# Turning a group's result tile by tile in four column groups of TensorE (graph layers, 4096 nodes)

## The chip, the cores and the metric

One Trainium2 chip; the program runs on one of its cores. The time is the device time of one execution in microseconds, and the median of the runs is quoted. Engines are named as in the profile: PE is TensorE (PEld its weight loads), DVE is VectorE, ACT is ScalarE, POOL is GpSimd, SP is SyncE, which here only issues DMA transfers.

## The reference

Two graph layers on 4096 nodes with 512 features, each on the layer norm of its input and added to it. The change lies in the second layer (layer 1), attention with 8 heads of 64 (argument names as in the call):

```python
# layer 0
h = jnp.maximum(_layernorm(x, axis=-1), 0.0)
node_att = jax.nn.softmax(h @ node_w, axis=0)
he = h @ edge_w
edge_att = jax.nn.softmax(jnp.where(adj > 0, he @ he.T, NEG_BIG), axis=1)
x = x + adj * (node_att * edge_att) @ (h @ weight) + bias
# layer 1
h = jnp.maximum(_layernorm(x, axis=-1), 0.0)
data1 = (h @ W.T + b).reshape(N, H, D)
src = jnp.einsum('nhd,xhd->nh', data1, src_proj)
trg = jnp.einsum('nhd,xhd->nh', data1, trg_proj)
e = src.T[:, :, None] + trg.T[:, None, :]
e = jnp.where(e >= 0, e, 0.01 * e)
e = e + adj[None, :, :]
scores = jax.nn.softmax(e, axis=-1)
out = jnp.einsum('hnm,hmd->hnd', scores, data1.transpose(1, 0, 2))
x = x + out.transpose(1, 0, 2).reshape(N, H * D)
```

So for each head and each of 4096 rows there is a weighted sum over 4096 neighbours and a denominator, and the result is their quotient plus the layer's input.

## The kernel before

Layer 0 takes the first 1580 us or so and isn't touched. Layer 1 works in eight **groups**: four blocks of 1024 rows (`WL`) times two halves of the heads (`HG` = 4 heads). A group has 32 **steps**, one for each tile of 128 neighbours (`m`, 0 to 31). The neighbours lie on the partitions and the rows along the free dimension, so the products come out turned: 128 partitions (head and feature) by rows.

The order is written out by hand (`manual_schedule`): line 1400 lists the stages of a step with how many steps ahead each works, and each engine and DMA queue runs its own instructions in the order in which they are issued. In step `s`:

- `load` (4 ahead): SP fetches a 128x1024 tile `e` of the adjacency.
- `exps` (1 ahead): ACT writes `ex`, the exponential of `e`, to PSUM. There is one buffer of `ex`, so ACT writes it only when DVE has read the one before.
- `rest`: at the first step of a group ACT copies what is left of the last group's sums out of PSUM (`copy_rest`, lines 1252 to 1258), after `os[0][0]` was copied at the end of `gather`.
- `weigh` (1 ahead): DVE forms the four heads' weights `pr` (lines 1171, 1174), in the order 3, 0, 1, 2 (`ORDER`). Head 3 uses `e3`, a second exponential; the others use `ex`. `pr` has two buffers for heads 1 to 3 and three for head 0. In one step of four (`BY_LOG`: m = 3, 7, ...) head 0's weights come from ACT and POOL (`lg`), and DVE has three products instead of four.
- `factors` (2 ahead): ACT writes `e3` (line 1114) and, for head 0, `rl` (line 1140), or `pr` from `lg` (line 1137) for a step in `BY_LOG`. `logs` (4 ahead) writes `lg` (line 1120).
- `scale`: in the first two groups, ACT (before, POOL) also multiplies two heads of the values by `d_m` (line 1100).
- `gather`: PE adds the step's products to the sums. Every product has a stationary operand at most 32 columns wide, so four products, one in each **column group** of 32 columns, go into the four quarters of PSUM's partitions: 16 products of values (line 1208, `pv`) and four of denominators (line 1213, `dn`). In the seven steps of `BY_HALF` one more product goes into a single column group; the order `cols` of the column groups is shifted by one after each, so that they go round. The last step adds nine products of sums that POOL and DMA have gathered (`acc`).

The **end of a group** is worked off during the next group by the generator `finish` (lines 1290 to 1318). `denominators` turns the 512 denominators' copy `od` and picks what is needed by four products with the matrix `pick` (line 1265); DVE takes the reciprocals `rd`. `turn` (lines 1278 to 1282) turns a row tile: two transposes of 128x128, with the whole width of PE. Two row tiles share one PSUM tile `pt` (one buffer). Then ACT scales each head's 64 columns with its share of `rd` into a tile `o` (line 1310, four instructions a row tile), POOL adds the layer's input by DMA (`due`, issued in `weigh` where m mod 4 is 1, from line 1154), and SP stores the two row tiles. `o` has two buffers, of which `od` takes one once a group.

`finish` is advanced by one `yield` in the steps of `PARTS` (lines 1013, 1415), counted in the next group: reciprocal products at 1, reciprocals and the first turn at 2, then, for each pair of row tiles, turns at 2, 6, 10 and 14, the scalings of one tile at 4, 8, 12, 16 and of the other at 5, 9, 13, 17, and the stores at 10, 14, 18 and 22. The last group ends in `finish_last` (lines 1321 to 1360), when nothing else runs: PE turns four tiles, forms the reciprocal products and turns the other four, and DVE and ACT share the scalings.

Of the kernel before, what the change touches and what calls it, by code (L numbers as in the profile page):

```python
# [8 lines left out]
FP = mybir.dt.float32  # L9
AF = mybir.ActivationFunctionType  # L10
ALU = mybir.AluOpType
# [4 lines left out]
P = 128  # L16
# [12 lines left out]
def kernel(  # L29
# [15 lines left out]
    nc = tc.nc  # L45
    N, F = x.shape
    H, D = 8, 64
    HG, WL = 4, 1024
    WT = WL // P
    NT = N // P  # L50
# [7 lines left out]
    ident = const.tile([P, P], FP, name="ident")  # L58
# [4 lines left out]
    x1 = dram.tile([N, F], FP, name="x1")  # L63
# [39 lines left out]
    with tc.tile_pool(name="w0", bufs=1) as wp, tc.tile_pool(name="a0", bufs=2) as ap_, tc.tile_pool(  # L103
        name="a0s", bufs=8
# [75 lines left out]
        def turn(t):  # L180
            b, j = divmod(t, TB)
            if j == 0:
                hts[b] = ap_.tile([P, KC, BL], FP, name="h_t")
            if t >= T0:
                nc.vector.transpose(
                    hts[b][:, :, j * P:(j + 1) * P].rearrange("p k (a q) -> p k a q", q=S),
                    hqs.pop(t).rearrange("p (a k q) -> p k a q", k=KC, q=S))
                return
            h = hs.pop(t)
            pt = pp.tile([P, KC, P], FP, name="bank")  # L190
            for k in range(KC):
                nc.tensor.transpose(pt[:, k, :], h[:, k * P:(k + 1) * P], ident)
            nc.vector.tensor_copy(hts[b][:, :, j * P:(j + 1) * P], pt)
            logit(t, h)
# [291 lines left out]
    with tc.tile_pool(name="mx0", bufs=1) as mx0, tc.tile_pool(name="b_b", bufs=3) as adj0, tc.tile_pool(  # L486
        name="mx1", bufs=1
    ) as mx1, tc.tile_pool(name="b_a", bufs=3) as adj1, tc.tile_pool(name="b_m", bufs=4) as mkp, tc.tile_pool(name="b_s", bufs=2) as sp, tc.tile_pool(
        name="b_p", bufs=6, space=PSUM
# [94 lines left out]
        for n in range(-5, len(items)):  # L584
# [3 lines left out]
            if n >= 0:  # L588
                i, j, t = items[n]
# [10 lines left out]
                if n in more:  # L600
                    f, m = more[n]
# [7 lines left out]
    with tc.tile_pool(name="c_x", bufs=1) as ldx, tc.tile_pool(name="c_y", bufs=1) as ldy, tc.tile_pool(  # L609
        name="c_d", bufs=2  # L610
    ) as wkp, tc.tile_pool(name="c_m", bufs=1) as mxp, tc.tile_pool(name="c_o", bufs=4) as iop, tc.tile_pool(
        name="c_s", bufs=2
    ) as sp, tc.tile_pool(name="c_q", bufs=1, space=PSUM) as p_q, tc.tile_pool(
        name="c_p", bufs=1, space=PSUM
# [12 lines left out]
        steps = [(n, q) for n in range(NB) for q in mixed(n)]  # L627
# [121 lines left out]
        left, scale, norms, zs = [], {}, iter(()), {}  # L749
# [25 lines left out]
        def denominators(n):  # L775
            b = ORDER_B[n]
            sc = sp.tile([P, TB], FP, name="sc")
            nc.vector.tensor_tensor(sc, zs.pop(n), dr[:, b * TB:(b + 1) * TB], ALU.add)
            nc.vector.reciprocal(sc, sc)
            nc.vector.tensor_tensor(sc, sc, na[:, b * TB:(b + 1) * TB], ALU.mult)  # L780
            scale[n] = sc
# [3 lines left out]
        def finish(n, j):  # L785

            b = ORDER_B[n]
            oc = iop.tile([P, F], FP, name="xt")
            blk[n][1].append(oc)
            for c, half in enumerate((2, 3) if j < 2 else (4, 5)):  # L790
                nc.scalar.activation(oc[:, c * F2:(c + 1) * F2], cs_[half][:, (j % 2) * F2:(j % 2 + 1) * F2], AF.Copy,
                                     scale=scale[n][:, j:j + 1])
            nc.gpsimd.dma_start(oc, xb_d[rows_of(b * TB + j), :], accum_op=ALU.add)
# [133 lines left out]
        for s in range(-5, end):  # L927
# [5 lines left out]
            n, q = steps[s]  # L933
# [28 lines left out]
        pt = bank(7)  # L962
# [45 lines left out]
    Q = P // 4  # L1008
# [1 line left out]

    PARTS = (0, 1, 2, 4, 5, 6, 8, 9, 10, 12, 13, 14, 16, 17, 18, 22)
    BY_LOG = (3, 7, 11, 15, 19, 23, 27, 31)
    BY_HALF = (4, 8, 12, 16, 20, 24, 28)
    BY_DMA = [m for m in range(NT - 1) if m not in BY_HALF]
# [2 lines left out]
    with tc.tile_pool(name="p", bufs=2) as prp, tc.tile_pool(name="s0", bufs=1) as s0, tc.tile_pool(  # L1019
        name="za", bufs=1  # L1020
    ) as zp0, tc.tile_pool(name="e", bufs=4) as ep, tc.tile_pool(name="p0", bufs=3) as pr0p, tc.tile_pool(name="rl", bufs=2) as rlp, tc.tile_pool(
        name="io1", bufs=2
    ) as iop, tc.tile_pool(name="s1", bufs=1) as sp, tc.tile_pool(name="e3", bufs=2) as e3p, tc.tile_pool(
        name="zb", bufs=1
    ) as zp1, tc.tile_pool(name="ac", bufs=2) as acp, tc.tile_pool(
        name="os", bufs=1
    ) as osp, tc.tile_pool(name="u", bufs=1) as usp, tc.tile_pool(
        name="p_x", bufs=1, space=PSUM
# [111 lines left out]
            nc.scalar.activation(r, zs_[i, 0], AF.Relu, bias=ngd_m[:, h // HG, m:m + 1], scale=d_m[:, h, m:m + 1])  # L1140
            rl[i, m] = r

        due = []

        def sums(i, m):
            if m < 2:
# [113 lines left out]
        def denominators(i):  # L1260
            os_, od = late.pop(i)
            yield os_
            pd = p_t.tile([P, JT, 2, 4], FP, name="pt")
            for j in range(JT):
                nc.tensor.matmul(pd[:, j, :, :].rearrange("p e r -> p (e r)"), od[:, j * P:(j + 1) * P],  # L1265
                                 pick.rearrange("p e r -> p (e r)"), start=True, stop=True)
            yield
            rd = sp.tile([P, JT, 2, 4], FP, name="rd", bufs=2)
            nc.vector.reciprocal(rd, pd)
            yield rd  # L1270

        def share(rd, t, r):
            q, j = divmod(t, JT)
            k = ORDER[r]
            e, r4 = (0, (k - 1) * HV + q) if k in (1, 2) else (1, (HV if k else 0) + q)
            return rd[:, j, e, r4:r4 + 1]

        def turn(os_, t, pt):
            q, j = divmod(t, JT)
            for c in range(2):  # L1280
                nc.tensor.transpose(pt[:, 2 * c:2 * c + 2, :].rearrange("p k d -> p (k d)"),  # L1281
                                    os_[c][q][:, j * P:(j + 1) * P], ident)

        def part(ap, i, t, n):

            b, g = groups[i]
            t += b * WT
            return ap[t * P:(t + n) * P, g * HG * D:(g + 1) * HG * D].rearrange("(j p) (h d) -> p j h d", p=P, h=HG)

        def finish(i):  # L1290


            dens = denominators(i)
            os_ = next(dens)
            yield
            next(dens)
            yield
            rd = next(dens)
            old = []
            for t in range(0, WT, 2):  # L1300
                pt = p_t.tile([P, 2, HG, D], FP, name="pt")
                for j in range(2):
                    turn(os_, t + j, pt[:, j, :, :])
                if t > 2:
                    nc.sync.dma_start(part(out, i, t - 4, 2), old.pop(0))
                yield
                o = iop.tile([P, 2, HG, D], FP, name="o")
                for j in range(2):
                    for r, k in enumerate(ORDER):
                        nc.scalar.activation(o[:, j, k, :], pt[:, j, r, :], AF.Copy, scale=share(rd, t + j, r))  # L1310
                    if j == 0:
                        yield
                old.append(o)
                due.append(lambda o=o, t=t: nc.gpsimd.dma_start(o, part(x1, i, t, 2), accum_op=ALU.add))
                yield
            nc.sync.dma_start(part(out, i, WT - 4, 2), old.pop(0))
            yield
            nc.sync.dma_start(part(out, i, WT - 2, 2), old.pop(0))
            yield

        def finish_last(i):

# [78 lines left out]
        for s in range(len(steps)):  # L1401
            for f, ahead in stages:
                if s + ahead < len(steps):
                    f(*steps[s + ahead])
                if s == 0 and f is exps:
                    early_logs(0, BY_LOG[0])
            if s == 0:
                ending = iter(())
            elif s == 2:
                ending = tables()  # L1410
            elif s % NT == 0:
                ending = finish(s // NT - 1)
            if s == len(steps) - 2:
                ending = finish_last(len(groups) - 1)
            if s < NT or s % NT in PARTS or s > len(steps) - 3:
                next(ending, None)
        for _ in ending:
            pass

# [33 lines left out]
```

## Time and profile before

| | us |
|---|---|
| median of 3 runs | 2805.27 (2805.01 to 2806.02) |
| the profiled execution, time | 2803.11 |
| its span in the profile | 2801.3 |
| layer 1's first product | 1603.0 |
| layer 1's last product of the main loop starts | 2790.2 |
| granted clock of PE over the span | 0.995 |

| group of instructions | count | mean of one, us |
|---|---|---|
| PE products of values, 128x512 (L1208) | 8192 | 0.594 |
| PE products of denominators with `d_m`, 128x512 (L1213) | 1984 | 0.592 |
| PE transposes `pt<-ident,os`, 128x128 (L1281) | 112 | 0.286 |
| PE reciprocal products `pt<-pick,o`, 128x8 (L1265) | 64 | 0.256 (median) |
| weight loads of 128x32 (L1208) | 8192 | 0.110 |
| weight loads of 128x128 (L1281 / L1265, median) | 112 / 64 | 0.140 / 0.192 |
| DVE `pr` from `ex` (L1174) | 512 | 1.271 |
| DVE `pr` from `e` (L1174) | 256 | 1.356 |
| ACT scalings `o<-pt,rd`, 128x64 (L1310) | 224 | 0.304 |

The span is one execution on the core, seen by the profiler; the time of that execution is 1.8 us more. Instructions on PE overlap: a product is listed with the time from its start to its modelled end, so their durations don't add up, and the distance from one start to the next tells the pace. A plain f32 product is listed as two instructions (4096 products of values in L1208). The same holds, less strongly, of DVE and ACT, where one instruction starts a little before the one before it ends. Times in the views are from the span's start. A bracket at a line's end is the engine's idle time just before it, and the instruction whose end ended it.

### The profile page before, as it was taken

The numbers are of one execution on the slowest core, as the hardware profiler recorded it, in microseconds if no ns is written. First come the engines' busy times: TensorE is split into PE (matmuls) and PEld (weight loads), VectorE is DVE, ScalarE is ACT, GpSimd is POOL, SyncE is SP. The second block draws the span as 40 slices with busy tenths as digits, with TensorE's granted clock in tenths as the row PEclk, the third lists the DMA queues.
The fourth block names the chain that finished last, engine by engine and source line by source line (L and its number), as shares of the span: only waits on it lengthen the run. The fifth ranks groups of instructions, "written<-read, shape, count | busy, mean of one in ns | idle before, by whom it ended". The sixth has DMA issues, their size and how long they took to land. (4 is left out here: it accounts for less than half of the span.)

```text
span 2801.3 us, 46750 instructions
## 1 busy us (share of the span) xinstructions
PE 2753.2 (98%) x16747; PEld 1499.1 (54%) x16747; DVE 2506.5 (89%) x3427; ACT 1475.5 (53%) x2218; POOL 1462.9 (52%) x1234
## 2 busy tenths in 40 slices
PE   7999999999999999999999899999999999999998
PEld 4885444444888888888885333323232323232322
DVE  7877799898888888888886799999999999999998
ACT  2212233333123333433332288998888888888786
POOL 5322344444011010111107698888978797979786
PEclk9999999999999999999999899999999999999999
DMA  5536898888889998999867279999999998989897
GB/s 175 176 104 244 285 330 301 303 297 269 202 200 201 214 262 188 232 251 218 230 193 195 84 193 241 239 229 240 220 241 228 241 231 236 225 244 224 218 218 172
DMA packets 535992, 629.85 MB, mean 225 GB/s; under 512 B 292152, under 2 KB 346456, under 8 KB 535760
## 3 DMA queue, kind: packets, MB, share of 16 engines
q1 hardware_dynamic: 461920, 415.87, 49.2%
q0 software_dynamic: 71824, 207.07, 34.1%
q10 hardware_dynamic: 2016, 3.93, 0.4%
q8 instruction: 131, 2.15, 0.3%
q14 instruction: 101, 0.83, 0.1%
HBM read 404.23 MB, written 107.15 MB: 183 GB/s over the span
## 5 line engine op out<-in xcount | busy, mean ns | idle before, releaser
L1208 PE MATMUL pv<-pr,sup 128*32 128x512 f32 x8192 | 1052.4, 594 | 9.7 <-DVE ngd_m L1163 5.5
L1174 DVE SCALAR_TENSOR_TENSOR pr<-z,g_m,ex 128x1024 f32<-128x1024 f32 x512 | 630.5, 1271 | 6.0 <-PE dn L1213 5.6
L1208 PEld LDWEIGHTS pv<-pr,sup 128*32 128x32 f32 x8192 | 306.7, 110 | 605.4 <-issue 564.3
L1185 POOL TENSOR_TENSOR acc<-acc,pr 128x1024 f32<-128x1024 f32 x240 | 576.0, 2400 | 100.4 <-DVE pr L1174 97.3
L531 PE MATMUL pe<-he_t,he_t 128*128 128x512 f32 x896 | 386.5, 592 | 0.0
L1213 PE MATMUL dn<-pr,d_m 128*2 128x512 f32 x1984 | 385.7, 592 | 0.0
L705 ACT ACTIVATE d<-d 128x1024 f32<-128x1024 f32 x126 | 133.1, 1056 | 430.8 <-DVE d L697 226.5
L1174 DVE SCALAR_TENSOR_TENSOR pr<-z,g_m,e 128x1024 f32<-128x1024 f32 x256 | 347.2, 1356 | 0.7 <-ACT e L1114 0.4
L1104 ACT ACTIVATE ex<-e 128x1024 f32<-128x1024 f32 x256 | 263.2, 1028 | 157.2 <-DVE pr L1174 156.1
L1114 ACT ACTIVATE e<-e,ld_m 128x1024 f32<-128x1024 f32 x256 | 291.1, 1137 | 0.0
L531 PEld LDWEIGHTS pe<-he_t,he_t 128*128 128x128 f32 x896 | 169.4, 190 | 208.3 <-issue 193.7
L744 PE MATMUL po<-he_t,at 128*128 128x256 f32 x1024 | 262.9, 379 | 1.0 <-ACT he_t L755 1.0
L744 PE MATMUL po<-sup,u 128*128 128x256 f32 x1024 | 263.3, 380 | 0.0
L1171 DVE SCALAR_TENSOR_TENSOR pr<-rl,ngd_m,ex 128x1024 f32<-128x1024 f32 x191 | 242.7, 1271 | 3.2 <-ACT ex L1104 2.6
L744 PE MATMUL po<-sup,at 128*128 128x256 f32 x1024 | 243.7, 381 | 1.0 <-DVE mc L537 1.0
L1140 ACT ACTIVATE rl<-z,ngd_m,d_m 128x1024 f32<-128x1024 f32 x191 | 234.8, 1229 | 0.0
L831 POOL DMA_DIRECT2D he_t<-he_t x56 | 48.7, 939 | 355.9 <-ACT he_t L747 301.9
L715 DVE TENSOR_TENSOR at<-d,a 128x1024 f32<-128x1024 f32 x126 | 154.1, 1223 | 84.0 <-PE po L744 46.3
L744 PEld LDWEIGHTS po<-sup,at 128*128 128x128 f32 x1024 | 195.7, 191 | 27.9 <-issue 1.2
L744 PEld LDWEIGHTS po<-he_t,at 128*128 128x128 f32 x1024 | 194.6, 190 | 27.6 <-issue 1.4
L744 PEld LDWEIGHTS po<-sup,u 128*128 128x128 f32 x1024 | 194.1, 190 | 25.9
L536 POOL DMA_DIRECT2D er_d<-mk x136 | 74.2, 546 | 234.0 <-DVE rm L533 217.8
(272 smaller groups left out, 3925.9 us busy)
## 6 DMA issues: line engine op xcount, KB each, us to landing
e<-in_adj_t_dram SPq DMA_DIRECT2D x256, 512.0 KB, 6.1
acc<-pr POOLq DMA_DIRECT2D x192, 512.0 KB, 6.4
a<-in_adj_t_dram SPq DMA_DIRECT2D x126, 512.0 KB, 5.0
ac<-in_adj_t_dram SPq DMA_DIRECT2D x124, 256.0 KB, 5.0
ar<-in_adj_dram SPq DMA_DIRECT2D x120, 256.0 KB, 4.7
ec_d<-mc POOLq DMA_DIRECT2D x120, 256.0 KB, 5.1
er_d<-mk POOLq DMA_DIRECT2D x112, 256.0 KB, 4.8
et<-er_d SPq DMA_DIRECT2D x448, 64.0 KB, 3.9
```

Source lines behind the costliest of these rows:

```text
L531: nc.tensor.matmul(pe[:, :w], he_t[i][:, k, (t % TB) * P:(t % TB + 1) * P], he_t[j][:, k, BL - w:], start=(k == 0), stop=(k == KC - 1))
L705: nc.scalar.activation(d, d, AF.Exp)
L715: nc.vector.tensor_tensor(w, d, aj.pop((n, q)), ALU.mult)
L744: nc.tensor.matmul(acc[:, j, :], A[:, j * P:(j + 1) * P], B, start=(first_ and j == 0), stop=last, skip_group_check=True)
L1104: nc.scalar.activation(x_, ra.pop((i, m)), AF.Exp)
L1114: nc.scalar.activation(x_, ra[i, m], AF.Exp, bias=ld_m[:, h // HG, m:m + 1])
L1140: nc.scalar.activation(r, zs_[i, 0], AF.Relu, bias=ngd_m[:, h // HG, m:m + 1], scale=d_m[:, h, m:m + 1])
L1171: nc.vector.scalar_tensor_tensor(w, rl.pop((i, m)), ngd_m[:, h // HG, m:m + 1], x_, op0=ALU.subtract, op1=ALU.mult)
L1174: p_ = nc.vector.scalar_tensor_tensor(w, zs_[i, k], g_m[:, h + k, m:m + 1], e3.pop((i, m)) if k == 3 else x_, op0=ALU.max, op1=ALU.mult)
L1185: nc.gpsimd.tensor_tensor(acc[i, 3], acc[i, 3], w, ALU.add)
L1208: nc.tensor.matmul(v[c][q][col * Q:(col + 1) * Q, :], va[:, m, g * HG + k, c0:c0 + Q], pr[i, m, k][:, q * BL:(q + 1) * BL], start=(m == 0) ...
L1213: nc.tensor.matmul(dn[col * Q:col * Q + w.shape[1], :], w, src, **fl)
```

## The change

The end of a group is no longer a generator that works by pairs of row tiles, but a function called in every step with the step's number since the group's end. Row tile t is turned in step `TURNS[t]` of the next group and scaled in the step after it. The pair's add of the input is made ready with the scaling of its second tile, and the store stands at a later step that is a multiple of 4: 12, 20, 28 and 32 with `TURNS`, 12, 20, 24 and 28 with `LAST_TURNS`, which the last group but one uses. 32 is the first step of the group after.

`turn` and `denominators` issue, in place of a product as wide as PE, four whose stationary operand is 32 columns wide, one in each column group. A turn is now a plain product with the unit matrix, not a transpose. Both functions are also used by `finish_last`.

```diff
-    PARTS = (0, 1, 2, 4, 5, 6, 8, 9, 10, 12, 13, 14, 16, 17, 18, 22)
+    TURNS = (3, 5, 9, 12, 16, 19, 23, 25)
+    LAST_TURNS = (3, 5, 9, 11, 15, 17, 21, 22)
...
             for j in range(JT):
-                nc.tensor.matmul(pd[:, j, :, :].rearrange("p e r -> p (e r)"), od[:, j * P:(j + 1) * P],
-                                 pick.rearrange("p e r -> p (e r)"), start=True, stop=True)
+                for c0 in range(0, P, Q):
+                    nc.tensor.matmul(pd[c0:c0 + Q, j, :, :].rearrange("p e r -> p (e r)"),
+                                     od[:, j * P + c0:j * P + c0 + Q],
+                                     pick.rearrange("p e r -> p (e r)"), start=True, stop=True)
...
             for c in range(2):
-                nc.tensor.transpose(pt[:, 2 * c:2 * c + 2, :].rearrange("p k d -> p (k d)"),
-                                    os_[c][q][:, j * P:(j + 1) * P], ident)
+                for c0 in range(0, P, Q):
+                    nc.tensor.matmul(pt[c0:c0 + Q, 2 * c:2 * c + 2, :].rearrange("p k d -> p (k d)"),
+                                     os_[c][q][:, j * P + c0:j * P + c0 + Q], ident, start=True, stop=True)
...
-        def finish(i):
...
+        def finish(i, m):
+
+            if m == 1:
+                got[i] = denominators(i)
+                turned[i] = next(got[i])
+                next(got[i])
+            if m == 2:
+                got[i] = next(got[i])
+            at = TURNS if i < len(groups) - 2 else LAST_TURNS
+            for t in range(WT):
+                j = t % 2
+                if j and m == ((at[t] + 1) // 4 + 2) * 4:
+                    nc.sync.dma_start(part(out, i, t - 1, 2), turned.pop((i, t - 1))[1])
+                if m == at[t]:
+                    if j == 0:
+                        turned[i, t] = p_t.tile([P, 2, HG, D], FP, name="pt"), iop.tile([P, 2, HG, D], FP, name="o")
+                    turn(turned[i], t, turned[i, t - j][0][:, j, :, :])
+                if m == at[t] + 1:
+                    pt, o = turned[i, t - j]
                     for r, k in enumerate(ORDER):
+                        nc.scalar.activation(o[:, j, k, :], pt[:, j, r, :], AF.Copy, scale=share(got[i], t, r))
+                    if j:
+                        due.append(lambda o=o, t=t: nc.gpsimd.dma_start(o, part(x1, i, t - 1, 2), accum_op=ALU.add))
...
-            elif s % NT == 0:
-                ending = finish(s // NT - 1)
+            for i in range(max(s // NT - 2, 0), s // NT):
+                finish(i, s - (i + 1) * NT)
             if s == len(steps) - 2:
                 ending = finish_last(len(groups) - 1)
-            if s < NT or s % NT in PARTS or s > len(steps) - 3:
-                next(ending, None)
+            next(ending, None)
```

More of the change, by code (lines that the diff above doesn't have):

```diff
@@ L1141, in relus @@
             rl[i, m] = r
-        due = []
+        due, got, turned = [], {}, {}
         def sums(i, m):
@@ L1288, in part @@
             return ap[t * P:(t + n) * P, g * HG * D:(g + 1) * HG * D].rearrange("(j p) (h d) -> p j h d", p=P, h=HG)
-        def finish(i):
[L1293 to L1308, printed above, removed]
-                    for r, k in enumerate(ORDER):
[L1310 to L1319, printed above, removed]
```

## The prediction

> **What bounds the kernel now.** The busy shares come first, then the stretch in which the change lies.
>
> ```profile
> PE 2753.2 (98%) x16747; PEld 1499.1 (54%) x16747; DVE 2506.5 (89%) x3427; ACT 1475.5 (53%) x2218; POOL 1462.9 (52%) x1234
> ...
> 2196.00:2345.00 149.00, 149.00 (x1356) 45.76 (x1351) 147.06 (x123) 122.24 (x143) 125.39 (x82) 1.00 0.92 234
> ```
>
> The second line is one stretch of layer 1 (length; then PE, PEld, DVE, ACT, POOL busy). PE is never idle and DVE lacks 1.9 us of 149, so two engines lie within two per cent of each other. The chain of waits says which ends last:
>
> ```profile
> 1915.56 0.99 PE pt L1265 x8
> 1916.55 3.57 PE pv L1208 x32
> 1920.12 0.86 PE dn L1213 x8
> 1920.98 0.59 PE pt L1281 x4
> ...
> 1938.85 0.86 PE dn L1213 x5
> 1939.71 0.59 PE pt L1281 x4
> ...
> 2652.04 0.99 PE pt L1265 x8
> ```
>
> It stays on PE from the second group to the end. L1265 comes once a group: (2652.04 - 1915.56)/5 = 147.30 us is a group's period. Four products, one in each column group, start together every 0.429 us (28 in 3.00); a step is ten such rounds, 4.29 us, and 32 steps are 137.3. What PE loses at a turn is seen in its timeline:
>
> ```profile
> 2380.15 0.59 PE L1208 MATMUL pv<-pr,sup 128*32 128x512 f32 x1
> 2380.16 1.44 PE L1213 MATMUL dn<-pr,d_m 128*2 128x512 f32 x5
> 2381.53 0.66 PE L1281 MATMUL pt<-ident,os 128*128 128x128 f32 x4
> 2382.11 1.92 PE L1208 MATMUL pv<-pr,sup 128*32 128x512 f32 x16
> ```
>
> Of the five denominator products three start with the round at 2380.15; the other two run alone, at 2380.58 and 2381.01, in the one column group that is behind, while three stand still: the full-width turn waits for all four.
>
> DVE waits for PE in few places; a step with a log (m = 7, 11, ...: one product fewer) shows it:
>
> ```profile
> DVE pr L1174 <- PE dn L1213: 1.0, 3, 0.5
> ...
> 2247.03 1.32 DVE L1174 SCALAR_TENSOR_TENSOR pr<-z,g_m,e 128x1024 f32<-128x1024 f32 x1
> 2248.85 2.47 DVE L1174 SCALAR_TENSOR_TENSOR pr<-z,g_m,ex 128x1024 f32<-128x1024 f32 x2 [0.50 <-PE dn L1213]
> 2251.24 1.28 DVE L1174 SCALAR_TENSOR_TENSOR pr<-z,g_m,e 128x1024 f32<-128x1024 f32 x1
> ```
>
> The first line is a whole group's. The step lasts 2251.24 - 2247.03 = 4.21 us, against 2324.23 - 2320.61 = 3.62 for a log step late in the group, where nothing holds DVE.
>
> **The change on PE, for one group.** Removed: the four reciprocal products with their bubble. From the last round before them to the first after, the stretch is 1.10 us longer than a round. Four turns of two tiles: 0.09 before the first (0.52 after the last round in place of 0.43), 0.59 until the next product, 0.02 for its visible weight load, 0.70 each, 2.8 in all. And part of the lost offset. Seven half products (BY_HALF) go round the column groups, two instructions of 0.43 each, 0.86. Turns at m = 6, 10, 14 pay one each and the four later ones share one: four times 0.86. With no full-width turn the most loaded column group has two: 1.72 saved. Together 5.6.
>
> Added: eight tiles, each eight products over 128 columns. A plain f32 product is two instructions (L1265: x64 for 32 products; L1281's transposes are one, x112), so a tile is 16 instructions or four rounds, a group 32 rounds. No row has so short a product in a column group. Bounds: 0.107 (0.429 x 128/512, the streaming alone) and 0.139 (as long as a 128-wide weight load, L1281's). I take 0.109, the spacing of L1281's own 128-column products: 3.5 us. The four reciprocal products of a group become sixteen, 32 instructions, eight rounds. Bounds: 0.03 a round (a load of 32 columns at the pace of L1265's 128, which take 0.112) and 0.110 (a whole 128x32 load); near the lower, 0.05: 0.4 us. PE then needs 147.3 - 5.6 + 3.5 + 0.4 = 145.6; between 145.3 and 147.0 by the bounds.
>
> The Trainium skill, TensorEngine Tiling (Array Packing), Instruction Overhead, speaks against cutting small products up: a product over one column costs what one over 60 does. By it a round of the 8-column products is an estimated 0.05 (0.429 x 60/512), the sum above stays; no row here has it. The same page, Restrictions, has column tiling exclude the f32 transpose mode, which is why these turns are products; were they one instruction, the 3.5 would be 1.75.
>
> **What is late next.** PE's gain counts only down to DVE's own period. Three log steps of a group last 4.08, 4.21 and 3.86 in place of 3.62, 1.29 together; a little of it is read differently by the waits view (1.0 idle), so I take 1.2: DVE alone needs 146.1.
>
> DVE's head 0 product in turn waits for ex, which has one buffer, and ACT writes it when the previous step has read it. ACT's spare before that write differs by step:
>
> ```profile
> 2322.72 1.23 ACT L1140 ACTIVATE rl<-z,ngd_m,d_m 128x1024 f32<-128x1024 f32 x1
> 2324.34 1.03 ACT L1104 ACTIVATE ex<-e 128x1024 f32<-128x1024 f32 x1 [0.39 <-DVE pr L1174]
> ...
> 2194.77 1.14 ACT L1120 ACTIVATE lg<-u,nlg_m 128x1024 f32<-128x1024 f32 x1
> 2195.81 1.00 ACT L1104 ACTIVATE ex<-e 128x1024 f32<-128x1024 f32 x1
> ...
> 1786.81 0.91 ACT L1310 ACTIVATE o<-pt,rd 128x64 f32<-128x64 f32 x4
> 1787.60 1.04 ACT L1104 ACTIVATE ex<-e 128x1024 f32<-128x1024 f32 x1
> ```
>
> In steps with s mod 4 = 2 (the next weighed step is the short one) rl to ex is 1.62; back to back it is 1.13: 0.49 spare. The same reading gives about 1.7 at 0, 1.15 at 1, 0.65 at 3. The four scalings of a tile cost 1787.60 - 1786.81 = 0.79. Before, they stand in steps 4, 5, 8, 9, 12, 13, 16, 17, mod 4 only 0 and 1, where they fit. After, they stand one step behind each turn: 4, 6, 10, 13, 17, 20, 24, 26. Steps 6, 10 and 26 are mod 2: 0.30 late each. The lg at 2194.77 is a like case, 1.04 into 0.49, so 0.55 late, and DVE idles 0.39 there (the view of its waits: ACT ex, once a group). So 0.30 gives DVE between 0 (if the e product before it covers it) and 0.30; I take 0.2, 0.6 a group. A full step is 146.1 + 0.6 = 146.7 on DVE, above PE's 145.6: 0.6 saved. The scalings now wait for a turn queued one step back, not two or three; behind them on ACT stands the next ex, for which DVE waits. PE starts a step's products at most 7.2 us after DVE's e product of that step (m = 16), so the turn is through 12 us after it (4.3 and 0.4 more); the scalings' turn on ACT comes 13 us after it (two steps and ex, e, rl). That 1 us is the cover; beyond it each us of lag would be DVE's. A second tile is turned into the other half of a pt that ACT may still read; only at step 22 of the last group do both fall together, and were the whole tile held, PE would wait for 0.8 once.
>
> **DMA queues.** As many as before. POOL's adds of x1 leave at steps 8, 16, 24, 28 in place of 8, 12, 16, 20; SP's stores at 12, 20, 28, 32 in place of 10, 14, 18, 22, three of four in the next steps behind loads for step s + 4. Each store comes four steps (18 us) after its add, which lands in 6.7 (median): SP doesn't wait there, and I cost it at nothing. Were a store late, the e tile queued behind it is four steps ahead of its use; without that cover up to 6.7 a store would be ACT's wait. The two o buffers come free as long before use.
>
> **The sum.** Groups 2 to 6: 5 x 0.6 = -3.0. Group 1 has another pair of scalings (L1100) in every ACT step, 0.48, which eats the 0.49 spare; 0.79 late three times, 0.6 each on DVE, less 0.3 of its wait for PE: +1.5. Group 7 has its tiles' scalings at 4, 6, 10, 12, 16, 18, 22, 23: four at mod 2 (0.8) and 0.05 at 23, less 1.2: -0.35. The last end is serial: eight turns and the reciprocal products stand before rd (2790.7 to 2792.6). Now four tiles of 0.44 and 0.4 to 0.9 come first, less the drain: rd 0.3 to 0.9 later, +0.6. In all -1.25: span 2801.3 to 2800.05. The profiled execution took 2803.11, its span plus 1.8; the median shown is 2805.27, 2.16 above. The difference carried to the median: 2804.0. With 0 to 0.3 for each late block, 2801 to 2807.
>
> **Rivals.** (1) ACT's late blocks cost nothing, because DVE's e products (1.28 to 1.38 against 1.19 apart) cover them: 5 x -1.2, group 1 -0.3, group 7 -1.2, end +0.6, -6.9: 2798.4. For it: the e product has some 0.1 to spare in most steps; against: the lg row. Chance 0.22. (2) Slower: the short products don't stream, each waits for its own weight load, 0.107 + 0.110 = 0.22 a round. PE: 145.6 + 32 x 0.11 = 149.1, +1.8 in seven groups, the end +2.4: 2820. It decides from 0.143 a round (where PE passes 146.7). For it: no such row; against: L1281 with wider loads keeps 0.109. Chance 0.14. (3) The change doesn't keep the offset: column groups still wait for each other at a turn, PE 147.3 again: 2806. Against: at the group start 2348.3 the groups run on separately. Chance 0.06. My forecast: 0.58.
>
> A measurement of this kernel tells 0.2% (5.6 us) from none. Faster than 2799.7: most of (1), a tail of mine, 0.23; slower than 2810.9: (2) and a little, 0.16; same 0.61. Range 2797.5 to 2815, which leaves out the worse half of (2) and the best of (1).
>
> **What would show it.** Right: the turn's rounds 0.11 apart with no single-product rounds before them; PE gaps before pv that end with DVE; DVE's wait for PE near 0 and for ex at steps 8, 12, 28; period 146.5 to 146.9. Wrong: rounds above 0.14, or DVE waiting for PE as before, or no wait for ex.

## The result and the profile after

The changed kernel takes 2811.54 us (median of 13 runs, 2808.58 to 2814.83), the kernel before in the same series 2805.37 (13 runs, 2803.41 to 2812.15): a ratio of 1.002, 95% interval 1.0012 to 1.0028. It is slower by about 6 us, where 1.25 us less were forecast. (One execution of e6, below, took 6067.75 us and the other three 2830.35 to 2834.50; its ratio is that of the three.)

The profiled execution took 2811.23 us, with a span of 2809.5, which is 8.2 more than before. Half of that is not the change's. Layer 0 is the same code in every kernel, and yet layer 1's first DVE product starts at 1605.56 here and at 1601.50 in the profile of before; in the twelve profiles of this study it starts anywhere from 1601.5 to 1610.3. So 4.06 us of the 8.2 are the spread of layer 0 between executions, and all that follows compares **layer 1 alone**, from that product to the end of the span: 1199.79 us before, 1203.90 after, +4.11. (The interval of the ratio is 3.4 to 7.9 us of 2805, so it holds this.)

Where it lies is read from the start of DVE's first `e` product in each group (us from one group's to the next, the last column to the end of the span):

| | group 0 | 1 | 2 | 3 | 4 | 5 | 6 | group 7 and end | layer 1 |
|---|---|---|---|---|---|---|---|---|---|
| before | 151.49 | 147.62 | 147.25 | 147.27 | 147.29 | 147.30 | 147.35 | 164.21 | 1199.79 |
| after | 151.47 | 149.03 | 146.48 | 147.23 | 147.69 | 147.70 | 147.67 | 166.63 | 1203.90 |
| difference | 0 | +1.4 | -0.8 | 0 | +0.4 | +0.4 | +0.3 | +2.4 | +4.1 |
| forecast | 0 | +1.5 | -0.6 | -0.6 | -0.6 | -0.6 | -0.6 | +0.25 | -1.25 |

That group 2 comes near its forecast is luck: PE takes 147.65 there too, from its first product of group 2 to that of group 3, and only falls back behind DVE, from 5.22 us after DVE's first product of the group to 6.39. From group 4 on, where it stands 6.9 behind, DVE has to wait for it. There the period is 147.7, and the page and one such group (length; then busy PE, PEld, DVE, ACT, POOL, with counts; clock, DMA share, GB/s) show which engine sets it:

```profile
PE 2760.3 (98%) x17835; PEld 1712.3 (61%) x17835; DVE 2509.7 (89%) x3427; ACT 1473.5 (52%) x2218; POOL 1462.1 (52%) x1234
...
2347.45:2495.15 147.70, 147.70 (x1478) 76.09 (x1474) 145.90 (x122) 120.39 (x142) 125.34 (x83) 1.00 0.93 232
```

PE is never idle over the whole group, while DVE lacks 1.8 us. The forecast had PE at 145.6 and DVE as the bound. The chain of waits (start, length, what) shows two turns of that group:

```profile
2372.16 0.86 PE dn L1214 x8
2373.01 0.44 PE pt L1285 x16
2373.45 3.43 PE pv L1209 x32
...
2381.98 0.14 PE dn L1214 x4
2382.12 0.13 PE pt L1285 x5
2382.25 0.59 PE dn L1214
2382.84 0.33 PE pt L1285 x9
2383.17 3.54 PE pv L1209 x30
```

L1285 is the turn's product. The turn of step 3 takes 0.44 us for its 16 instructions, 0.109 a round as forecast. The turn of step 5 comes after the first half product (step 4), which has left one column group 0.86 behind, and there the chain goes through a lone denominator product, 0.59, while the turn stands. PE's timeline (start, length, instruction) tells why:

```profile
2381.41 1.00 PE L1214 MATMUL dn<-pr,d_m 128*2 128x512 f32 x4
2381.84 0.42 PE L1285 MATMUL pt<-ident,os 128*32 128x128 f32 x6
2382.25 0.59 PE L1214 MATMUL dn<-pr,d_m 128*2 128x512 f32 x1
2382.68 0.49 PE L1285 MATMUL pt<-ident,os 128*32 128x128 f32 x9
2382.93 0.61 PE L1209 MATMUL pv<-pr,sup 128*32 128x512 f32 x3
```

At 2381.84 three column groups are free and start two short instructions each (one product, since a plain f32 product is two instructions). Then nothing starts in them until 2382.68, when the fourth is through its last denominator at 2382.25 plus 0.43. From 2382.68 on the fourth runs its four, with the rest of the others beside it. So at a turn the column groups do wait for each other, for part of the offset.

How far the free ones get depends on the order of issue. Counted from the starts in the trace, they run what was issued before the second short product of the group behind, and then nothing until that group starts its first. That is six instructions where it stands first in the order 0 to 3 (steps 5 and 23), eight where it is second (9 and 25), ten where it is third (12) and twelve where it is last (16), the same in each of the groups 2 to 6. Measured from the start of PE's products of one step to that of the next, with 4.29 for a plain step, the eight turns of a group (the one before; this one differs by 0.01) cost:

| step | 3 | 5 | 9 | 12 | 16 | 19 | 23 | 25 | sum |
|---|---|---|---|---|---|---|---|---|---|
| PE's step | 4.73 | 5.38 | 5.17 | 5.36 | 5.36 | 4.73 | 5.39 | 5.18 | |
| over 4.29 | 0.44 | 1.09 | 0.88 | 1.07 | 1.07 | 0.44 | 1.10 | 0.89 | 6.98 |

Six of the eight find a column group behind; each pays 0.44 to 0.66 beside its 0.44, together 3.5 us. At steps 12 and 16 the group behind comes 0.2 late from the turn before, beside its half product; so step 16 costs 1.07 although twelve instructions get ahead. Before, the four turns of two tiles cost 5.32 by the same reading (5.01 and three of 5.82).

The table leaves out the reciprocal products. They meet the same loss: in the changed kernel the column groups come to them up to 0.6 apart, and PE's step 1 takes 5.58, against 4.59 in e3 (below), where all four come together.

What ACT's new places cost is seen in DVE's waits (engine, line, waited for: us in all, times, longest), first in group 1, then in group 5:

```profile
DVE pr L1172 <- ACT ex L1105: 2.3, 4, 0.6
...
DVE pr L1172 <- ACT ex L1105: 0.7, 2, 0.4
DVE pr L1175 <- PE dn L1214: 0.7, 2, 0.4
```

In group 1, where ACT also multiplies values, DVE's steps 8, 12 and 28 last 5.54, 5.53 and 5.54 in place of 4.77, 4.78 and 4.82: 0.7 to 0.8 each. The step after each is 0.1 shorter and step 19, which had waited for PE, 0.3, which leaves about the +1.4. Before, it waited 0.4 for ACT in that group.

### The profile page after: what moved, and what is told of

The parts are those of the page before. It is cut to its first block, busy times and chain, and to the rows that moved or that the text cites. A ratio compares the mean times of both kernels' runs of the same rounds, so it can differ in the third digit from the quotient of the medians.

```text
span 2809.5 us, 48930 instructions
## 1 busy us (share of the span) xinstructions
PE 2760.3 (98%) x17835; PEld 1712.3 (61%) x17835; DVE 2509.7 (89%) x3427; ACT 1473.5 (52%) x2218; POOL 1462.1 (52%) x1234
## 5 line engine op out<-in xcount | busy, mean ns | idle before, releaser
L1209 PEld LDWEIGHTS pv<-pr,sup 128*32 128x32 f32 x8192 | 460.1, 110 | 436.7 <-issue 233.4
L1214 PE MATMUL dn<-pr,d_m 128*2 128x512 f32 x1984 | 378.7, 592 | 0.0
```

Source lines behind the costliest of these rows:

```text
L1209: nc.tensor.matmul(v[c][q][col * Q:(col + 1) * Q, :], va[:, m, g * HG + k, c0:c0 + Q], pr[i, m, k][:, q * BL:(q + 1) * BL], start=(m == 0) ...
L1214: nc.tensor.matmul(dn[col * Q:col * Q + w.shape[1], :], w, src, **fl)
```

## The experiments

All compare layer 1 alone by their profile, and their median with runs of the kernel before made on the same chip. Layer 1 by groups, in us:

| | group 1 | 4 | 5 | 6 | group 7 and end | layer 1 | turns on PE | ratio, 95% interval |
|---|---|---|---|---|---|---|---|---|
| before | 147.62 | 147.29 | 147.30 | 147.35 | 164.21 | 1199.8 | 5.3 | |
| after | 149.03 | 147.69 | 147.70 | 147.67 | 166.63 | 1203.9 | 7.0 | 1.002, 1.0012 to 1.0028 |
| e1, order of the column groups | 149.05 | 146.77 | 146.53 | 146.48 | 166.03 | 1199.7 | 6.0 | 1.0007, 0.9999 to 1.0016 |
| e2, steps alone | 149.11 | 150.12 | 150.13 | 150.12 | 168.81 | 1219.2 | 8.9 | 1.0067, 1.0053 to 1.0081 |
| e3, quarter products alone | 147.81 | 146.51 | 146.60 | 146.53 | 163.72 | 1196.6 | 5.3 | 0.9988, 0.9979 to 0.9997 |
| e4, last group's turns earlier | 149.05 | 147.71 | 147.68 | 147.72 | 166.49 | 1203.9 | 7.0 | 1.0018, 1.0009 to 1.0028 |
| e5, e3 with late scalings | 150.20 | 146.74 | 146.72 | 146.68 | 163.87 | 1199.5 | 5.3 | 1.0008, 0.9999 to 1.0018 |
| e6, e3 with half products moved | 153.32 | 149.25 | 149.65 | 149.81 | 167.15 | 1225.9 | 3.5 | 1.0093, 1.0076 to 1.0110 |
| e7, before with half products moved | 151.14 | 149.79 | 149.74 | 150.57 | 166.78 | 1224.2 | 2.8 | 1.0090, 1.0075 to 1.0105 |
| e8, order and fitting steps | 147.79 | 146.25 | 146.40 | 146.38 | 163.59 | 1195.0 | 5.2 | 0.9992, 0.9982 to 1.0001 |
| e9, fitting steps alone | 147.72 | 147.04 | 147.01 | 147.06 | 164.25 | 1198.6 | 5.9 | 0.9997, 0.9987 to 1.0006 |
| e10, e8 again | 148.11 | 146.35 | 148.01 | 146.23 | 163.59 | 1196.5 | 5.2 | 0.9992, 0.9983 to 1.0001 |

("turns on PE" is group 4's sum over 4.29 a step, as in the table of step 3 to 25 above.)

### e1: the turn's products in the order in which the column groups come free

```diff
-                for c0 in range(0, P, Q):
+                for c0 in [(n + u) % 4 * Q for u in range(4)]:
                     nc.tensor.matmul(pt[c0:c0 + Q, 2 * c:2 * c + 2, :].rearrange("p k d -> p (k d)"),
...
+    turn(turned[i], t, ..., sum(u <= m for u in BY_HALF) % 4)
```

> The changed kernel, with the four products of a turn issued in the order of the column groups that the next step uses, not always 0 to 3. Theory A (a turn's fixed order makes the column groups that are ahead wait for the one that is behind): a turn then costs 0.44 us of PE at any step, PE needs 147.7 - 5 x 0.65 = 144.4 a group, and DVE with ACT bounds at 146.5 to 146.9; from layer 1's start to the end 4 to 6 us less than in the changed kernel. Theory B (the short products are dear in themselves): turns keep costing about 1.1 and the period stays at 147.7. Theory C (the scalings in steps with s mod 4 = 2 set the period): 147.7 too, now with waits of DVE for ex in each group.

The period fell to between 146.5 and 146.8, and layer 1 by 4.2 us, with nothing but the order of issue changed. So the fixed order is a cause. It isn't the whole loss: the 0.44 at any step and the 144.4 a group of theory A did not come. PE takes 146.8 a group here and still falls back by 0.3 a group behind DVE, which sets the 146.5. PE's timeline at the same turn:

```profile
2379.99 1.00 PE L1214 MATMUL dn<-pr,d_m 128*2 128x512 f32 x4
2380.42 0.63 PE L1285 MATMUL pt<-ident,os 128*32 128x128 f32 x12
2380.83 0.59 PE L1214 MATMUL dn<-pr,d_m 128*2 128x512 f32 x1
2381.26 0.27 PE L1285 MATMUL pt<-ident,os 128*32 128x128 f32 x1
2381.26 0.63 PE L1209 MATMUL pv<-pr,sup 128*32 128x512 f32 x3
```

Now the three free column groups run all twelve of their short instructions from 2380.42. Their next products, the long ones of the next step, start only at 2381.26, together with the fourth's first short one. So the offset is still lost, but partly filled: a turn out of step costs 5.14 to 5.16 in place of 5.17 to 5.39, and 0.42 of the 0.86 remain as loss, six times a group. Twelve start ahead at each of the six turns here, as they did in the changed kernel where the group behind was last in the order. Why the reach ends there these runs don't show.

The Trainium skill has a rule that would exclude what these rows show. TensorE: Matmul & The Clock Gate, Part 3: Packing small matmuls, says that matmuls start and end strictly in program order. In e1 the lone denominator product that starts at 2380.83 was issued before all twelve short instructions, the first of which start at 2380.42; and the fourth group's first short instruction, at 2381.26, was issued before six of the twelve, the last of which starts at 2380.78. Across column groups, starts pass each other here, and the measurement decides.

With PE's need down, DVE shows ACT's late blocks: its steps 8, 12 and 28 last 5.08, 5.06 and 5.06, against 4.82, 4.77 and 4.82 in e8, where no block is late. The step after each is 0.11 to 0.13 shorter (4.77 against 4.88 to 4.90), so a late block costs about 0.15, where 0.2 had been taken. The last group stays long, 166.03.

### e2: the new steps, with products of full width

```diff
-                for c0 in range(0, P, Q):
-                    nc.tensor.matmul(pt[c0:c0 + Q, ...], os_[c][q][:, j * P + c0:j * P + c0 + Q], ident, ...)
+                nc.tensor.transpose(pt[:, 2 * c:2 * c + 2, :]..., os_[c][q][:, j * P:(j + 1) * P], ident)
```

The reciprocal products are of full width too.

> The changed kernel's steps for turns, scalings, adds and stores, but with the full-width transposes and reciprocal products of before. Theory A: eight full-width turns of one tile, each with its bubble (0.09 + 0.22 + 0.2) and with the offset lost at about five of them, so no better than the changed kernel: 147.5 to 148.3 a group. Theory B: the short products gone, 147.3 or less. In the first group with turns and in the last the same losses as in the changed kernel (+1.4 and about +2), since they belong to the steps.

150.12 us a group, more than the 147.5 to 148.3 expected: eight turns where four stood, and six of them find a column group behind. PE's timeline at step 5:

```profile
2394.01 0.59 PE L1209 MATMUL pv<-pr,sup 128*32 128x512 f32 x1
2394.01 1.44 PE L1214 MATMUL dn<-pr,d_m 128*2 128x512 f32 x5
2395.39 0.44 PE L1282 MATMUL pt<-ident,os 128*128 128x128 f32 x2
2395.76 3.64 PE L1209 MATMUL pv<-pr,sup 128*32 128x512 f32 x32
```

As in the kernel before, the two lone denominators run out before the turn starts: nearly the whole 0.86 is lost. Its steps cost 4.78 in step and 5.61 out of it, 8.9 in all against 7.0 for the quarter products in the same steps. That is 1.9 of the 2.4 between 150.12 and 147.70; the step with the reciprocal products costs another 0.6 (6.21 against 5.58), and the last step gives 0.2 back (6.03 against 6.24).

### e3: quarter products in the kernel before

The two functions `turn` and `denominators` of the changed kernel, in the generator, steps and stores of the kernel before.

```diff
+                for c0 in range(0, P, Q):
+                    nc.tensor.matmul(pd[c0:c0 + Q, j, :, :]..., od[:, j * P + c0:j * P + c0 + Q], pick..., ...)
...
+                for c0 in range(0, P, Q):
+                    nc.tensor.matmul(pt[c0:c0 + Q, ...], os_[c][q][:, j * P + c0:j * P + c0 + Q], ident, ...)
```

> The kernel before, its steps unchanged, with the quarter-width products alone. Theory A: turns of two tiles at 2, 6, 10, 14 in fixed order, 0.87 each and some 0.65 lost at three of them; reciprocal products 1.2: 147.3 to 147.8 a group. Theory B: the same 5.6 us of full-width work replaced by dearer products, above 148. The first group with turns back at 147.6 and no stall of 2 us in the last, if these belong to the steps.

The products are the good half of the change, and better than the 147.3 to 147.8 expected: layer 1 is 3.2 us shorter than before, and this is the only kernel whose interval lies wholly below 1. PE's timeline at the reciprocal products and at two turns, the first in step, the second not:

```profile
2364.79 0.47 PE L1266 MATMUL pt<-pick,o 128*32 128x8 f32 x31
2365.09 0.61 PE L1208 MATMUL pv<-pr,sup 128*32 128x512 f32 x1
...
2369.40 1.09 PE L1284 MATMUL pt<-ident,os 128*32 128x128 f32 x32
2370.27 3.65 PE L1208 MATMUL pv<-pr,sup 128*32 128x512 f32 x32
...
2387.46 0.42 PE L1284 MATMUL pt<-ident,os 128*32 128x128 f32 x6
2387.87 0.59 PE L1213 MATMUL dn<-pr,d_m 128*2 128x512 f32 x1
2388.30 0.93 PE L1284 MATMUL pt<-ident,os 128*32 128x128 f32 x25
```

The gain is in the first of them. The 32 reciprocal instructions stand 0.30 before the next product (2364.79 to 2365.09), 0.04 a round; PE's steps 0 and 1 of a group together take 9.7 to 9.8 where they took 10.5. The turns gain nothing: steps 5.19, 5.82, 5.62 and 5.81, 5.3 over plain steps as before. Two tiles of short products take 0.87, a turn of full width 0.70 to 0.72, and the loss out of step is 0.46 to 0.66 in place of 0.83: the one eats the other. PE catches up with DVE late in each group (from DVE's `e` product of step 31 to PE's products of it 2.81, after 4.26), so DVE sets 146.5.

### e4: the last group's turns earlier

```diff
-    LAST_TURNS = (3, 5, 9, 11, 15, 17, 21, 22)
+    LAST_TURNS = (3, 5, 9, 11, 15, 17, 19, 21)
```

> The changed kernel with the last two turns of the last group at 19 and 21 in place of 21 and 22, so that POOL's last add has two steps between the scaling and its issue. Theory D (POOL waits for ACT's scaling there, and with it the log step's sum, ACT and DVE): the stall of about 2 us in step 26 of the last group goes, 1.5 to 2 us in all; the other groups as in the changed kernel. If the stall has another cause it stays.

In the last group of the changed kernel POOL, ACT and DVE stand in turn, by its waits and, last, the timelines of POOL and DVE:

```profile
ACT pr L1138 <- POOL lg L1130: 6.1, 7, 2.6
...
POOL o L1316 <- ACT e L1115: 2.2, 1, 2.2
...
2764.46 1.73 POOL L1130 TENSOR_TENSOR lg<-lg,e 128x512 f32<-128x512 f32 x1
2763.82 3.46 DVE L1175 SCALAR_TENSOR_TENSOR pr<-z,g_m,e 128x1024 f32<-128x1024 f32 x1
```

POOL's add for the last pair waits 2.2; the row names ACT's `e`, the second instruction after the late scaling. DVE's product lasts 3.46 in place of 1.35, and its step 26 is 6.96. In e4, where the scaling comes earlier, that is gone, as expected: DVE's steps run through, and the longest of ACT's waits for POOL is 0.6. Yet nothing is gained, 166.49 against 166.63. In the changed kernel PE starts the products of step 26 only 5.4 us after DVE's first product of it, and those of step 27, after the stall, 2.75 after: its delay covered DVE's 2 us. So two paths end together: with the stall PE follows DVE at 2.73 in step 31, as before the change, and without it (e4) PE itself is last, 3.43 behind. Where PE isn't behind, the stall should cost: e1 has the same `LAST_TURNS` and takes 166.03 from group 7 on, e8 and e10, with no late turn, 163.59. That pair differs in other steps too, so the 2.4 is not the stall's alone by these runs.

### e5: e3 with ACT's scalings, and all turns but the first pair's, one step later

```diff
-    PARTS = (0, 1, 2, 4, 5, 6, 8, 9, 10, 12, 13, 14, 16, 17, 18, 22)
+    PARTS = (0, 1, 2, 5, 6, 7, 9, 10, 11, 13, 14, 15, 17, 18, 19, 22)
```

> The kernel before with the quarter-width products and with each pair's turns (but the first) and all scalings one step later: scalings at 5, 6, 9, 10, 13, 14, 17, 18, so four of eight in steps with s mod 4 = 2. If a scaling there makes ex late (0.79 into 0.49 of spare): DVE idles about 0.25 for ex at steps 8, 12, 16, 20, and the period rises from 146.55 to 147.2 to 147.6; in the first group with turns about 0.7 each, near 150.5 for 147.8. If DVE's e products cover it: no wait for ex beyond the one a group, 146.5 to 146.8.

Four of the eight scalings now stand in steps where they don't fit. Group 1 grows from 147.81 to 150.20, 0.6 for each of four late blocks, as priced. Groups 4 to 6 grow by 0.1 to 0.2 only, less than four blocks of 0.2. DVE's steps 8, 12, 16 and 20 are 5.07, 4.96, 5.06 and 5.05, up to 0.25 late each; but its log steps, which PE had held at 3.86 and 3.83 in e3, are now 3.72 and 3.64. What DVE loses to ACT it would otherwise have waited for PE.

### e6 and e7: all turns in step

The half products moved behind the turns, e6 with quarter products, e7 with the turns of the kernel before:

```diff
-    BY_HALF = (4, 8, 12, 16, 20, 24, 28)
+    BY_HALF = (16, 17, 18, 20, 24, 26, 28)
```

> The kernel before with the quarter-width products, and with the seven half products at 16, 17, 18, 20, 24, 26, 28 in place of 4, 8, ..., 28, so that no column group is behind when a pair is turned (2, 6, 10, 14). Theory A (the loss at a turn is the offset): the steps with a turn last 4.29 + 0.87 and no more (5.82 and 5.62 with the halves between them), DVE no longer waits for PE, 146.0 to 146.4 a group. If the loss belongs to the products: 5.6 to 5.8 as before and 146.55.

> The kernel before, full-width turns and all, with the half products moved alone (16, 17, 18, 20, 24, 26, 28). Theory A: a turn costs its 0.70 and no idle rounds, PE needs 147.3 - 1.7 = 145.6, DVE bounds at 146.1 to 146.5: most of what the quarter width brings, without it. If the width is what costs: 147.3 as before.

On PE the theory holds to a hundredth: with no column group behind, a step with a turn of two tiles takes 5.16 in e6 (4.29 and eight rounds of 0.109) and 4.99 in e7 (4.29 and 0.70); the first of a group takes 0.03 more. Quarter products are then dearer than full ones; all that they can win is the offset.

The times went the other way, layer 1 by 24 (e7 against before) and 29 us (e6 against e3), and not at a turn: in e6's group 5 DVE's steps 19, 20 and 28 take 4.65, 5.78 and 5.78, in e3's 3.81, 4.77 and 4.82, which is 2.8 of the 3.0 us between the groups. Timelines of POOL and DVE in e6 at steps 18 to 20:

```profile
2300.34 2.27 POOL L1191 TENSOR_TENSOR acc<-acc,pr 128x512 f32<-128x512 f32 x1
2302.56 1.28 POOL L1129 TENSOR_TENSOR lg<-lg,e 128x512 f32<-128x512 f32 x1
2303.80 2.38 POOL L1185 TENSOR_TENSOR acc<-acc,pr 128x1024 f32<-128x1024 f32 x1
2306.14 2.29 POOL L1191 TENSOR_TENSOR acc<-acc,pr 128x512 f32<-128x512 f32 x1
2308.39 2.39 POOL L1185 TENSOR_TENSOR acc<-acc,pr 128x1024 f32<-128x1024 f32 x1
...
2304.95 2.32 DVE L1174 SCALAR_TENSOR_TENSOR pr<-z,g_m,e 128x1024 f32<-128x1024 f32 x1
2307.20 2.46 DVE L1174 SCALAR_TENSOR_TENSOR pr<-z,g_m,ex 128x1024 f32<-128x1024 f32 x2
2309.58 2.27 DVE L1174 SCALAR_TENSOR_TENSOR pr<-z,g_m,e 128x1024 f32<-128x1024 f32 x1
```

A step with a half product gives POOL one more sum, L1191. Three such steps in a row, with a log beside them, fill POOL without a gap, and L1191 takes 2.27 in place of its 1.28. DVE's product for head 3, which writes a buffer that POOL's sum L1185 reads, ends 1.1 after that sum each time (2306.18 and 2307.27; 2310.78 and 2311.85) and lasts 2.3 in place of 1.3. It looks as if it waited for that buffer, but the profile names no release inside an instruction, and one row speaks against it: in the changed kernel's last group the product of 3.46 ends at 2767.28, also 1.1 after a sum of POOL, and that sum (L1130, up to 2766.19, shown under e4) reads no `pr`. What makes both engines slow here stays open.

### e8, e9 and e10: both causes taken away

e8 and e10 are e1 with the scalings in the steps 4, 5, 8, 9, 12, 13, 16 and 17, where they stood in the kernel before; e9 has those steps and the fixed order.

```diff
-    TURNS = (3, 5, 9, 12, 16, 19, 23, 25)
-    LAST_TURNS = (3, 5, 9, 11, 15, 17, 21, 22)
+    TURNS = (3, 4, 7, 8, 11, 12, 15, 16)
+    LAST_TURNS = TURNS
```

> The changed kernel with turns in the column groups' order and with turns at 3, 4, 7, 8, 11, 12, 15, 16, so scalings at 4, 5, 8, 9, 12, 13, 16, 17, in the steps where ACT has room. Against the same order with the changed kernel's steps (146.5 to 146.8 a group, 149.05 in the first with turns): no waits of DVE for ex but the one at a group's start, 147.7 in the first group, 146.1 to 146.5 after it. If the scalings' steps don't matter: 149 and 146.6 again.

> The changed kernel with turns at 3, 4, 7, 8, 11, 12, 15, 16 (scalings where ACT has room) and the turns' fixed order 0 to 3 of the column groups. If both causes hold and add up: no waits of DVE for ex, so the first group with turns at 147.6 to 148 in place of 149.03, but PE still loses 0.4 to 0.65 at the turns that are out of step (4, 7, 8, 11, 12, 15), so 146.6 to 147.7 a group, above the 146.3 of the same steps with the order that follows the column groups. If the steps alone mattered: 146.3 here too.

> The version with both mended (order of the column groups, scalings where ACT has room) once more, timed beside the kernel before and the one above: layer 1 in the profile within 0.5 us of 1195.0, against 1199.8 before and 1203.9 in the changed kernel; the median 3 to 5 us under that of before.

Both causes hold and nearly add up: layer 1 is 4.2 us under the changed kernel's in e1, 5.3 in e9 and 8.9 in e8. e9 mends group 1 (147.72, as before) and has only four turns out of step, of 5.18 to 5.40: 5.9 on PE and 147.0 a group. e8 with the order as well has 5.2 and 146.3. DVE's waits in e8, group 5:

```profile
DVE pr L1172 <- ACT ex L1105: 0.4, 1, 0.4
DVE pr L1175 <- PE dn L1214: 0.2, 1, 0.2
```

Only the lateness that the kernel before had is left. Layer 1 takes 1195.0 us in e8, the shortest of all, and 1196.5 in e10, where it had been expected within 0.5 of 1195.0; its median is 2.6 us under that of before in place of 3 to 5.

These steps bring a wait of their own. ACT scales the third pair from step 12 on into the first pair's buffer `o`, whose store leaves in that same step. Over layer 1 of e8, ACT's waits for stores are

```profile
ACT o L1314 <- DMA out_dram<-o: 9.1, 11, 1.7
```

and none is listed before or in the changed kernel. In e10's group 5 the store left at 2401.91 and landed at 2411.15; the scaling started at 2411.25, after 2.8 us of waiting. (The view names a denominator product of PE there; e8's scaling at the same place starts before that product does, so it isn't needed.) PE's next turn waited for that scaling, and its step took 6.39 in place of 5.16.

In time e8 and e10 are at 0.9992 with intervals that just touch 1; e3, which changes nothing but the two functions, has 0.9988 and a layer 1 of 1196.6. Which of e3 and e8 is better these runs can't tell.

## Why the prediction was wrong

The forecast was 2804.0, 0.2% slower came out: 7.5 us above it, and inside the range. That it lies inside is luck: the upper end was drawn for rival (2), dear short products, which isn't what happened. Against its own sum in layer 1, -1.25 forecast and +4.1 measured, the error is 5.4 us: 3.3 in groups 2 to 6, 2.2 in group 7 and the end, the rest small.

**The failed step** is this term of PE's sum: "With no full-width turn the most loaded column group has two: 1.72 saved." It took the column groups to run on apart past a quarter-width turn, as they do past the products of a step. They don't. Six of the eight turns find one column group behind, the three others run six to twelve short instructions and stop, and 3.5 us a group are lost where 1.72 were allowed. The turns cost PE 7.0 in place of 5.2, and its period is 147.7 in place of 145.6. e1, which changes the order of issue only, gives 0.9 of it back on PE and up to 1.2 of the period; e6 and e7, where no column group is behind, lose nothing at a turn.

Two more terms of that sum were off, and they partly cancel. The reciprocal products, taken at 0.4, lose the offset too: step 1 is 1.29 over a plain step. And the 147.3 that the sum starts from wasn't all PE's own need, though PE's busy share hides it. Before, PE waited at the start of each group for ACT to copy the last sums out of PSUM; in the changed kernel, from group 3 on, it comes too late to wait (the first line is before, the second after, over all groups from the second on):

```profile
PEld pv L1208 <- ACT os L1255: 6.4, 13, 0.8
PEld pv L1209 <- ACT os L1256: 1.9, 3, 0.8
```

Before, PE's step 0 took 5.04, some 0.75 more than a plain one. An estimate of its own need then is 147.30 - 0.75 = 146.55, from which the forecast's terms would have given 144.9. Of the 2.8 up to 147.7, 1.8 are the turns and 0.9 the reciprocal products.

**Rival (3)** named this and had a chance of 0.06. The row held against it, column groups running on separately at the start of a group, was of long products issued in the order in which the groups come free. The turn issues short ones in the order 0 to 3, and e1 shows that with short ones part of the offset goes even in the other order. And the rival was itself sized at the old 147.3: it gave four losses of 0.86, not six of 0.44 to 0.66.

**The prices of the new products were right.** A round of 128 columns takes 0.109, as taken (16 instructions in 0.44). A round of 8 columns takes 0.04 where the column groups are in step (0.30 for eight, in e3), near the 0.05 taken. Rival (2), 0.22 a round, is out. The Trainium skill's 60 cycles for the smallest product, from which the prediction worked out an estimated 0.05 a round (TensorEngine Tiling (Array Packing), Instruction Overhead), is a little more than the 0.04 measured here.

**ACT's late blocks were right.** Group 1 grew by 1.4 where 1.5 were forecast; where PE doesn't cover them (e1), each late block costs DVE about 0.15 in place of 0.2. Rival (1), that they cost nothing, is out for these groups. In the changed kernel itself they hardly count from group 4 on, because PE ends last there: the forecast had the two engines the wrong way round.

**The last group was wrong twice.** It was forecast at -0.35 and took 2.2 more up to its last step. The late scaling at steps 22 and 23 was seen as PE waiting 0.8 at most; with it POOL stood 2.2 and DVE 2, a wait that the prediction didn't follow to POOL's queue. PE's loss and this stall lie side by side: taking the stall away (e4) gains 0.1, because PE is then last, so either alone makes up nearly all of the +2.4, and it can't be split between them. The serial end came out a little under its forecast: from the last denominator product to `rd` 0.2 more, for 0.3 to 0.9.

**DMA queues** cost nothing, as forecast: in the waits of SP's queue the stores stood 16.6 us for their adds before, in all groups together, and none after, and no engine waits for an `e` tile.

## What to carry to other kernels

A product of full width makes all column groups wait for the one behind; cutting it into four doesn't free them. It only lets those ahead run a few short products further, and the most, twelve instructions here, where the group behind comes last in the order of issue. So first count how many turns meet a column group that is behind: four joint turns lost less here than eight single ones, and moving work to finer steps multiplied the loss. And before moving an engine's work to other steps, list that engine's spare time step by step, also for the next queue down (POOL behind ACT), since what doesn't fit in a step comes back as a wait elsewhere.

## What the runs showed that was not expected

- Between executions layer 0 ends anywhere in a stretch of 8.8 us (1601.5 to 1610.3), although its code is the same in all twelve profiles. One profile's span can't tell changes of a few us; a stage measured from its own first instruction can, to within about 1.5 us (e8 against e10, the 1.5 being the store's wait in e10).
- Column groups start products out of the order of issue, but with a limited reach: up to the second waiting product of the group that is behind, then nothing until that group starts its first. Here that is 6, 8, 10 or 12 short instructions, by its place in the order; e3's turns at steps 6, 10 and 14 give 6, 8 and 10 as well. With a step's long products one product is 0.86, as much as a half product leaves behind, and there nothing is lost (4.29 a step); that the reach counts products and not time is a reading of this that no run tests.
- POOL's sum of 128x512 took 2.27 in place of 1.28 when POOL had no gap (e6); why is open.
